# A block transpose of values, moved along VectorE's queue in a multi-query attention layer

## The chip, the cores and the metric

The kernel runs on one core of one Trainium2 chip. A core has engines that run side by side, each with its own queue of instructions that it takes in order: TensorE (PE, matrix products; its weight loads are shown as PEld), VectorE (DVE), ScalarE (ACT), GpSimd (POOL) and SyncE (SP), which here issues nearly all transfers. The engines tell each other by semaphores when something is done. The metric is device time in microseconds (us) of one execution; the runs before lie within 0.16 us of each other, so tenths of a microsecond can be read.

## What is computed

`x` holds 64 batches of 128 tokens with 512 numbers each. Each token row is normalised; 16 query heads of 64 numbers are projected from it, and one pair of keys and values that all heads share. A null key and value, taken from `cond`, stands ahead of the others. Scores get a bias and two masks, go through a softmax, weigh the values, are projected back, normalised and added to `x`.

```python
xn = layernorm(x, g_in)
q = (xn @ Wq).reshape(b, n, H, DH).transpose(0, 2, 1, 3) * scale
kv = xn @ Wkv
k, v = (kv[..., :DH], kv[..., DH:])
...
sim = jnp.einsum('bhid,bjd->bhij', q, k)
sim = sim + bias
...
attn = jax.nn.softmax(sim, axis=-1)
out = jnp.einsum('bhij,bjd->bhid', attn, v)
out = out.transpose(0, 2, 1, 3).reshape(b, n, INNER)
out = out @ Wo
return layernorm(out, g_out)
```

The outer function returns `x` plus this.

## The kernel before

**Groups and pairs.** Batches are worked in groups of four (`g`, 16 of them) and in pairs (`d`, 32 of them, with batches `a = 2d` and `b = 2d + 1`). The schedule is written out by hand: each engine gets its instructions in the order in which the Python code calls the helpers. For each pair there is a `turn(d)`, which makes the scores of the pair and the values products of the pair before (`p = 2d - 2`), and then a `body(d)`, for d from 1 to 29. The last two pairs have `turn_end` and `body_end`.

**What a body does.** Body d works on four things at once. It runs the softmax of pair d (`exps` on ScalarE, `rinv` on VectorE, `scale` on GpSimd, then `blocks_T`, a large transpose on VectorE that makes the weights of the values products). It projects the output of pair d - 1 (`out_product`, `out_part`), and normalises, adds and stores the output of pair d - 2 (`pair_stats`, `pair_nmr`, `pair_norm`, `pair_gain`, `pair_residual`). It makes keys, values and queries of the group after the next scores, `g = d // 2 + 1`: an even body (`h = 0`) does the first half of this group, an odd body (`h = 1`) the second. And it prepares token rows of group `g + 1`, as long as there is one (`norm_stats`, `norm_nmr`, `norm_apply`, `tokens_T`, then `tokens_out` and `tokens_in`, a round through DRAM that leaves the tokens transposed in `xT`).

**Keys and values.** `kv_pair` (L363) makes keys and values of two batches in one product `pkv`, keys in the lower 64 partitions, values in the upper. `kv_pair_out` reads it: VectorE takes the values into `vT` (L380), ScalarE the keys into `kT` (L390), and SP copies the keys to the other 64 partitions (L396). When the second pair of a group is through, `values_T(g)` brings the four batches' values into rows: VectorE transposes `vT` in blocks of 32 by 32 into `vb` (L401), SP writes `vb` to DRAM in two transfers (`vd`, L406) and reads it back in four (`vr`, L411). `values` (L781, tiles `po`) reads `vr` in the turns of that group.

**Queries.** The query projection is done by a scheme of seven products in place of eight: `product(g, f, k, ...)` (L515) makes product k for feature block f; both blocks f0 and f1 of a body use the same two rooms in PSUM, `pa` and `pc`. Products 1, 6, 7, 4 go into `pa` one on top of the other, products 5 and 3 into `pc`; between them, `keep` (ScalarE, L527) and `q_out` (VectorE L536, or ScalarE L533) read what stands there. Product 5 opens a new tile in `pc` and so needs the last reading of the old one done. Product 2 is again split into seven small ones, `inner_product` (L581, tile `pl`), read by `inner_out` (VectorE, L597), from d = 2 on; body 1 makes product 2 as a whole instead, and then prepares the summed weights for the small ones in `weight_sums_inner` (L554).

**Order on VectorE in an odd body.** The values (L380), the transpose `vb` (L401), then the readings of the norms: `pair_nmr` (L919), `norm_stats` (L270 to L280); then score maxima, gains and residuals (L929, L932) with the query readings between them, `tokens_T` (L326), two readings of small products (L597), the reciprocal `rinv(a, 1)` (L701), two more readings, `blocks_T(a)` (L721) and so on. An even body has the same order without `vb`.

**Order on SP in an odd body.** Keys copy, `vd` twice, `vr` four times, two stores (L935), `xd` (L335), `xT` four times (L343), two `res` (L131), two `x` (L122).

Of the kernel before, what the change touches and what calls it, by code (L numbers as in the profile page):

```python
# [17 lines left out]
def kernel(  # L18
# [356 lines left out]
    def kv_pair_out(m, pkv):  # L375
        g, t = divmod(m, GB)
        if t == 0:
            vTs[g] = hp.tile([P, GB, N], FP, tag="kv", name=f"vT_{g}", bufs=1)
        two = slice(t, t + 2)
        nc.vector.tensor_scalar(  # L380
            vTs[g][V_ROWS, two],
            pkv[V_ROWS].rearrange("p (t n) -> p t n", t=2),
            nkv[V_ROWS],
            None,
            ALU.subtract,
        )
        src = pkv[K_ROWS].rearrange("p (t i q) -> p t i q", t=2, i=NQ)
        out = kT[K_ROWS, :, two].rearrange("p i t q -> p t i q")
        for at, to, n in ((0, 0, 2), (3, 2, 1), (2, 3, 1)):
            nc.scalar.activation(  # L390
                out[:, :, to : to + n],
                src[:, :, at : at + n],
                AF.Identity,
                bias=nkv_neg[K_ROWS],
            )
        nc.sync.dma_start(out=kT[V_ROWS, :, two], in_=kT[K_ROWS, :, two])  # L396

    def values_T(g):

        vb = hp.tile([P, GB * NQ, Q], FP, tag="vb", name=f"vb_{g}", bufs=1)  # L400
        nc.vector.transpose(  # L401
            vb[V_ROWS], vTs[g][V_ROWS].rearrange("p t (j q) -> p (t j) q", q=Q)
        )
        vd = dp.tile([Q, GB * NQ, DH], FP, tag="vd", name=f"vd_{g}")
        for at in range(0, DH, Q):
            nc.sync.dma_start(  # L406
                out=vd[:, :, at : at + Q], in_=vb[DH + at : DH + at + Q]
            )
        vr[g] = hp.tile([P, GB, NQ, DH], FP, tag="vr", name=f"vr_{g}")
        for s in range(NQ):  # L410
            nc.sync.dma_start(  # L411
                out=vr[g][s * Q : (s + 1) * Q].rearrange("p t j d -> p (t j) d"),
                in_=vd,
            )
# [114 lines left out]
    def q_out(g, c, h, tag, name=None):  # L529
        o = q_part(g, c, h)  # L530
        p = prod[tag].rearrange("p (t h i) -> p t h i", t=2, h=2)
        if name is None:
            nc.scalar.copy(o, p)  # L533
        else:
            k = kept.pop(name).rearrange("p (t h i) -> p t h i", t=2, h=2)
            nc.vector.tensor_tensor(o, p, k, ALU.add)  # L536
# [10 lines left out]
    def weight_sums_inner():  # L547
        for o, p, m, op in (
            (r1, d21, d22, ALU.add),
            (r2, r1, d11, ALU.subtract),  # L550
            (r4, d12, r2, ALU.subtract),
            (r3, d11, d21, ALU.subtract),
        ):
            nc.vector.tensor_tensor(o, p, m, op)  # L554
# [10 lines left out]
    def inner_product(g, h, k):  # L565

        if k == 1:
            inner[g, h] = ps_w.tile([P, 4, N], FP, tag="w", name=f"pl_{g}_{h}")
        lo = xT[g][:, 0 : GB // 2]
        x = xL.get(g)  # L570
        t1, t3, t2, t4 = (x if x is None else x[:, i] for i in range(4))
        w, t, at = {
            1: (d11, lo[:, 0, HK], 0),
            2: (d12, lo[:, 0, KC - 1], 2),
            3: (r4, lo[:, 1, KC - 1], 1),
            4: (d22, t4, 0),
            5: (r1, t1, 1),
            6: (r2, t2, 0),
            7: (r3, t3, 0),
        }[k]  # L580
        nc.tensor.matmul(  # L581
            inner[g, h][:, at],
            w[:, h],
            t,
            start=k == 1,
            stop=True,
            skip_group_check=k != 1,
        )

    def inner_out(g, h, f, t, at, name=None):  # L590

        o = q_part(g, 2 * h + f, 0)[:, t]
        p = inner[g, h][:, at].rearrange("p (h i) -> p h i", h=2)
        k = o
        if name is not None:
            k = kept[name].rearrange("p (t h i) -> p t h i", t=2, h=2)[:, t]
        nc.vector.tensor_tensor(o, p, k, ALU.add)  # L597
# [80 lines left out]
    def exps(b, hf, lo=0, hi=R8):  # L678
        if hf == 0 and lo == 0:
            rsum[b] = small.tile([P, 2, R8], FP, tag="rsum", name=f"rsum_{b}")  # L680
        for k in range(lo, hi):
            row = S[b][:, k, WITH_NULL[hf]]
            nc.scalar.activation(  # L683
                row,
                row,
                AF.Exp,
                bias=nmax[b][:, hf, k : k + 1],
                accum_out=rsum[b][:, hf, k : k + 1],
            )
# [8 lines left out]
    def rinv(b, hf, lo=0, hi=R8):  # L698
        if lo == 0:
            rinvs[b, hf] = small.tile([P, R8], FP, tag="rinv", name=f"rinv_{b}_{hf}")  # L700
        nc.vector.reciprocal(rinvs[b, hf][:, lo:hi], rsum[b][:, hf, lo:hi])  # L701

    def scale(b, hf, lo=0, hi=R8):
        sv = S[b][:, lo:hi, KEYS[hf]]
        nc.gpsimd.tensor_tensor(  # L705
            sv,
            sv,
            rinvs[b, hf][:, lo:hi].unsqueeze(2).broadcast_to([P, hi - lo, sv.shape[2]]),
            ALU.mult,
        )  # L710
# [534 lines left out]
    def body(d):  # L1245

        a, b, p, l = 2 * d, 2 * d + 1, 2 * d - 2, 2 * d - 4
        g, h = d // 2 + 1, d % 2
        q, soft = g < NG, d > 0
# [20 lines left out]
            token_sum(g, 3)  # L1270
        if q:
            kv_pair_out(g * GB + 2 * h, pkv)
            if h == 1:
                values_T(g)
        if h == 0 and g + 1 < NG:
            load_mask(g + 1)
        if ln:
# [102 lines left out]
        if deep:  # L1380
            inner_product(g, h, 7)
            inner_out(g, h, 1, 1, 0, "p1")
            inner_out(g, h, 1, 1, 1)
        elif q:
            q_out(g, f1, 0, "w", "p1")
            weight_sums_inner()
        if soft:
            exps(a, 1, 4)
            rinv(a, 1)
            scale(a, 1)  # L1390
            exps(b, 1, 0, 2)
# [184 lines left out]
    for d in range(1, PAIRS - 2):  # L1576
        turn(d)
        body(d)
# [42 lines left out]
```

## Time and profile before

| | us |
|---|---|
| median of three runs | 1029.53 (1029.39 to 1029.55) |
| the profiled execution, its own time | 1029.77 |
| its span | 1027.9 |
| 16 transposes `vb`, each | 0.71 |

The page gives the busy time of each engine and the chain of work that ended last. The lists of groups give the mean duration of an instruction by line and operation. The chain in order of time has a start, a length and what ran; the timelines have a start, a duration, the engine, the line, what is written and read, and in brackets how long the engine stood idle before and who released it. Successive instructions of VectorE overlap slightly, so a start can lie a little ahead of the end before it. Busy time of PE is modelled at its ends: a product that is held back shows as a longer piece of the chain, not as idle time.

### The profile page before, as it was taken

To read this page: it belongs to the slowest core of one execution; us is meant where nothing else is said; L and a number is where in the kernel's file an instruction comes from. 1 tells how busy PE (TensorE), PEld (TensorE's weight loads), DVE (VectorE), ACT (ScalarE), POOL (GpSimd) and SP (SyncE) were. 2 spreads that over 40 slices of the span, in tenths; PEclk is the share of its full clock that TensorE was granted. 3 is DMA by queue.
4 is the path that set the end of the run, shared out by engine and by line. 5 is a ranking of instruction groups with operands and counts; after the bars stand their busy time and mean duration, and the time that the engine had idled before them with its cause. 6 is when DMAs were issued, how large, how long until landed. Compare 5 with 4: busy or idle time off the path is not lost.

```text
span 1027.9 us, 31287 instructions
## 1 busy us (share of the span) xinstructions
PE 1018.8 (99%) x12345; PEld 899.6 (88%) x12345; DVE 799.0 (78%) x1774; ACT 699.1 (68%) x2805; POOL 745.2 (72%) x579
## 2 busy tenths in 40 slices
PE   9999999999999999999999999999999999999997
PEld 9888888888888888888888888888888888888886
DVE  6877777877778877788777788777888777877697
ACT  5766678666678666786666786666776667856582
POOL 4997768686686857758677686776868678586676
PEclk9999999999999999999999999999999999999999
DMA  6514152141522315233141421415223151230211
GB/s 212 144 56 127 66 152 87 53 129 64 163 77 92 99 59 167 68 108 114 45 150 67 134 99 49 140 63 158 83 76 108 60 172 69 94 90 25 82 63 63
DMA packets 73834, 100.85 MB, mean 98 GB/s; under 512 B 32212, under 2 KB 36056, under 8 KB 71896
## 3 DMA queue, kind: packets, MB, share of 16 engines
q1 hardware_dynamic: 73392, 98.47, 30.8%
q8 instruction: 96, 1.57, 0.6%
q14 instruction: 50, 0.41, 0.1%
q10 hardware_dynamic: 296, 0.40, 0.1%
HBM read 63.19 MB, written 33.55 MB: 94 GB/s over the span
## 4 chain that ended last, share of the span: by engine, by line
PE 97%; DVE 1%; POOL 1%; issue 0%; POOLq 0%; DVEq 0%
PE pa L515 20%; PE pyX L868 19%; PE pyY L868 10%; PE pc L515 10%; PE po L781 7%; PE pkv L363 6%; PE pyw L868 5%; PE pl L581 4%; PE pq L450 3%; PE ps L652 3%; PE sc_X L652 2%; PE sc_Y L652 2%; PE py_s L868 1%; PE sc_a L652 1%; PE sc_w L652 1%; PE busy L1453 1%
## 5 line engine op out<-in xcount | busy, mean ns | idle before, releaser
L683 ACT ACTIVATE s<-s,nmax 128x65 f32<-128x65 f32 (+1 forms) x1024 | 372.0, 367 | 62.4 <-DVE nmax L674 62.4
L705 POOL TENSOR_TENSOR s<-s,rinv 128x512 f32<-128x512 f32 (+1 forms) x132 | 190.8, 1448 | 151.0 <-DVE rinv L701 151.0
L617 POOL TENSOR_TENSOR s<-biasp,mneg 128x1552 f32<-128x1552 f32 (+1 forms) x65 | 205.9, 3171 | 51.2 <-DVE s L667 38.2
L683 ACT ACTIVATION_READ_ACCUMULATOR s<-s,nmax 128x1 f32 x1024 | 194.6, 190 | 0.0
L533 ACT COPY qT<-pa 128x256 f32<-128x256 f32 x59 | 22.0, 373 | 147.2 <-PE pa L515 147.2
L674 DVE TENSOR_REDUCE nmax<-s 128x8 f32<-128x1032 f32 (+1 forms) x128 | 121.4, 949 | 0.1
L515 PE MATMUL pa<-xS,wq 128*128 128x256 f32 x472 | 121.2, 379 | 0.0
L721 DVE STREAM_TRANSPOSE sb<-s 128x1536 f32<-128x1536 f32 (+1 forms) x68 | 113.5, 1672 | 2.0 <-POOL s L705 2.0
L868 PE MATMUL pyX<-wT,oT 128*128 128x256 f32 x464 | 109.7, 379 | 0.0
L868 PE MATMUL pyX<-wo,oT 128*128 128x256 f32 x464 | 109.7, 379 | 0.0
L515 PEld LDWEIGHTS pa<-xS,wq 128*128 128x128 f32 x472 | 87.2, 190 | 11.1 <-issue 0.2
L868 PEld LDWEIGHTS pyX<-wo,oT 128*128 128x128 f32 x464 | 86.0, 190 | 10.5
L868 PEld LDWEIGHTS pyX<-wT,oT 128*128 128x128 f32 x464 | 85.9, 190 | 10.6
L848 POOL TENSOR_TENSOR oT<-oT 128x512 f32<-128x512 f32 x64 | 80.6, 1277 | 3.9 <-PE pyw L868 1.6
L781 PE MATMUL po<-sb,vr 32*64 32x256 f32 (+1 forms) x4064 | 81.4, 300 | 0.0
L781 PEld LDWEIGHTS po<-sb,vr 32*64 32x64 f32 x4064 | 70.9, 130 | 8.4 <-issue 5.3
L597 DVE TENSOR_TENSOR qT<-pl,kp 128x128 f32<-128x128 f32 x112 | 31.2, 279 | 58.6 <-PE pl L581 56.0
L800 ACT ACTIVATE oT<-po,nv 128x512 f32<-128x512 f32 (+1 forms) x127 | 73.7, 654 | 0.1
L536 DVE TENSOR_TENSOR qT<-pc,ku 128x256 f32<-128x256 f32 x118 | 48.5, 411 | 32.5 <-PE pc L515 18.1
L281 POOL TENSOR_TENSOR rstd<-rstd,nhalf 128x1 f32<-128x1 f32 x64 | 35.1, 555 | 52.5 <-DVE rstd L280 43.6
L363 PE MATMUL pkv<-xT,wkv 128*128 128x256 f32 x256 | 63.3, 391 | 0.0
L527 ACT COPY ku<-pa 128x256 f32<-128x256 f32 x118 | 43.4, 368 | 28.3 <-PE pa L515 23.8
(186 smaller groups left out, 2419.2 us busy)
## 6 DMA issues: line engine op xcount, KB each, us to landing
res<-in_x_dram SPq DMA_DIRECT2D x64, 256.0 KB
x<-in_x_dram SPq DMA_DIRECT2D x63, 256.0 KB
out_dram<-y SPq DMA_DIRECT2D x63, 256.0 KB
xd<-xb SPq DMA_DIRECT2D x14, 1024.0 KB
xT<-xd SPq DMA_DIRECT2D x56, 256.0 KB
vr<-vd SPq DMA_DIRECT2D x64, 128.0 KB
kT<-kT SPq DMA_DIRECT2D x32, 64.0 KB
vd<-vb SPq DMA_DIRECT2D x32, 64.0 KB
```

The lines of the kernel that those rows point to most:

```text
L363: nc.tensor.matmul(pkv, wkv[:, kc, :], xT[g][:, t : t + 2, kc, :], start=(kc == 0), stop=(kc == KC - 1),)
L515: nc.tensor.matmul(prod[tag], w[:, kc, f * P : (f + 1) * P], t[:, :, kc, :], start=(start and kc == 0), stop=(kc == HK - 1), skip_group_ch ...
L617: nc.gpsimd.tensor_tensor(S[b][:, :, keys], biasp[:, :, keys], mneg[:, t, keys] .unsqueeze(1) .broadcast_to([P, R8, keys.stop - keys.start ...
L652: nc.tensor.matmul(home[r][u * DH : (u + 1) * DH, f, :], qT[g, f, t // 2][rows, t % 2, hf, u], kT[rows, 0 : nk // Q, t, :], start=True, st ...
L674: nc.vector.tensor_reduce(nmax[b][:, hf], S[b][:, :, WITH_NULL[hf]], AX.X, ALU.max, negate=True)
L683: nc.scalar.activation(row, row, AF.Exp, bias=nmax[b][:, hf, k : k + 1], accum_out=rsum[b][:, hf, k : k + 1],)
L705: nc.gpsimd.tensor_tensor(sv, sv, rinvs[b, hf][:, lo:hi].unsqueeze(2).broadcast_to([P, hi - lo, sv.shape[2]]), ALU.mult,)
L721: nc.vector.transpose(sbs[b][:, :, lo:hi].rearrange("p j e q -> p e j q"), S[b][:, lo:hi, 1 : ROW - 1].rearrange("p e (j k) -> p e j k", k=Q),
L781: nc.tensor.matmul(po[s][rows, to : to + n], vr[g][quad, t, PLACE[j], :], sb[quad, slots, r * NF : (r + 1) * NF, :], start=(turn == 0), st ...
L800: nc.scalar.activation(to, src, AF.Identity, bias=nv2)
L848: eng.tensor_tensor(o, a, b, op)
L868: nc.tensor.matmul(prod[key], h[:, c, :], w[:, c, :], start=(start and c == 0), stop=(c == HC - 1), skip_group_check=not start,)
```

## The change

The call of `values_T(g)` moves within `body`. It stood directly behind `kv_pair_out`; now it stands behind the two readings of small product 7 (or, in body 1, behind `weight_sums_inner`), ahead of `exps(a, 1, 4)`, `rinv(a, 1)` and `scale(a, 1)`. Its transpose takes that place in VectorE's queue, and its six transfers come behind the two `x` loads in SP's. The call for group 0, ahead of the first turn, stays. Nothing else is changed.

```diff
@@ body
         if q:
             kv_pair_out(g * GB + 2 * h, pkv)
-            if h == 1:
-                values_T(g)
         if h == 0 and g + 1 < NG:
             load_mask(g + 1)
@@ body
         elif q:
             q_out(g, f1, 0, "w", "p1")
             weight_sums_inner()
+        if q and h == 1:
+            values_T(g)
         if soft:
             exps(a, 1, 4)
             rinv(a, 1)
```

## The prediction

> **What bounds the kernel now.** I read the page first: how full each engine is, and what the chain that ended last consists of.
>
> ```profile
> span 1027.9 us, 31287 instructions
> PE 1018.8 (99%) x12345; PEld 899.6 (88%) x12345; DVE 799.0 (78%) x1774; ACT 699.1 (68%) x2805; POOL 745.2 (72%) x579
> PE 97%; DVE 1%; POOL 1%; issue 0%; POOLq 0%; DVEq 0%
> ```
>
> TensorE is busy for 1018.8 of 1027.9 us and makes up 97% of the chain. A change on VectorE can pay only where it shortens something that PE itself counts as busy. So I cut the steady state into whole periods, from one keys product to the next, and asked for the busy time of each engine in them (columns: window, length, then each engine's busy time with its count, PE clock, DMA share, GB/s).
>
> ```profile
> 160.24:191.47 31.23, 31.23 (x384) 27.63 (x383) 24.29 (x56) 22.27 (x89) 23.55 (x20) 1.00 0.16 56
> 191.47:222.86 31.39, 31.39 (x383) 27.70 (x383) 24.90 (x57) 21.35 (x87) 21.75 (x16) 1.00 0.47 142
> 222.86:254.09 31.23, 31.23 (x384) 27.62 (x383) 24.29 (x56) 22.29 (x89) 23.54 (x20) 1.00 0.16 57
> ```
>
> PE is busy all through, at full clock. The first and third windows start with an even body (d = 4, 6), the second with an odd one (d = 5). Both issue the same PE work, yet the odd one takes 0.16 to 0.17 us longer. VectorE executes one instruction more there (57 against 56, 24.90 against 24.29 us): `values_T`. The chain of waits, in order of time, says where the extra time sits (start, length, what).
>
> ```profile
> 172.78 0.86 PE pc L515 x4
> ...
> 141.38 1.04 PE pc L515 x4
> ...
> 204.00 1.04 PE pc L515 x4
> ...
> 892.86 1.04 PE pc L515 x4
> ...
> 955.48 0.87 PE pc L515 x4
> ```
>
> It is one piece: product 5 of the second feature block on `pc`, 0.86 us in an even body and 1.04 in an odd one. From 141.38 (d = 3) to 892.86 (d = 27) every odd body has a piece of 1.03 or 1.04, thirteen in all. Body 29 (955.48) has none; it reads no more tokens, so VectorE has less in front. Body 1, with its own branch, has none either. What holds the piece is in the instruction timelines.
>
> ```profile
> 170.88 0.68 DVE L932 TENSOR_TENSOR y<-yn,res 128x512 f32<-128x512 f32 x1
> 171.73 0.42 DVE L536 TENSOR_TENSOR qT<-pc,ku 128x256 f32<-128x256 f32 x1 [0.17 <-PE pc L515]
> 172.61 1.03 PE L515 MATMUL pc<-xS,wS 128*128 128x256 f32 x4
> ...
> 193.96 0.71 DVE L401 STREAM_TRANSPOSE vb<-vT 64x512 f32<-64x512 f32 x1
> 202.84 0.68 DVE L932 TENSOR_TENSOR y<-yn,res 128x512 f32<-128x512 f32 x1
> 203.44 0.41 DVE L536 TENSOR_TENSOR qT<-pc,ku 128x256 f32<-128x256 f32 x1
> 203.91 1.13 PE L515 MATMUL pc<-xS,wS 128*128 128x256 f32 x4
> ```
>
> Product 5 opens a new tile in the slot of `pc`, so it waits until `q_out` (L536) has read the old one. In the even body `q_out` waits 0.17 us for PE: VectorE is early. In the odd body it stands directly behind the residual L932 with no idle time: VectorE is late, ends at 203.85, and PE starts at 203.91.
>
> **The change part by part.** *The early place (13 odd bodies, d = 3 to 27).* The transpose leaves the place at 193.96. Everything behind it on VectorE comes up to 0.71 us earlier, until it meets an input. That is the queue of the even body, whose `q_out` starts at 171.73; one 31.23 us period later is 202.96, against 203.44 now. In the even body it ends at 172.15, 0.46 us before PE comes at 172.61, so the stall goes: 1.04 - 0.86 = 0.17 to 0.18, and 31.39 - 31.23 = 0.16 from the windows. I take 0.17: 13 x 0.17 = 2.2 us gained. Nothing can yield more here, since the period of the even body has the same PE work.
>
> *The new place in these bodies.* The transpose now follows the second reading behind small product 7 and precedes the reciprocal `rinv(a, 1)`.
>
> ```profile
> 173.58 0.29 DVE L597 TENSOR_TENSOR qT<-pl,qT 128x128 f32<-128x128 f32 x1
> 174.59 0.20 DVE L701 RECIPROCAL rinv<-rsum 128x8 f32<-128x8 f32 x1 [0.72 <-ACT s L683]
> 174.87 1.91 POOL L705 TENSOR_TENSOR s<-s,rinv 128x1024 f32<-128x1024 f32 x1 [1.19 <-DVE rinv L701]
> 177.12 1.77 DVE L721 STREAM_TRANSPOSE sb<-s 128x1536 f32<-128x1536 f32 x1
> ...
> 205.82 0.20 DVE L701 RECIPROCAL rinv<-rsum 128x8 f32<-128x8 f32 x1 [0.25 <-ACT s L683]
> 211.16 0.42 DVE L536 TENSOR_TENSOR qT<-pc,ku 128x256 f32<-128x256 f32 x1 [0.46 <-ACT ku L527]
> ```
>
> In the even body, VectorE is idle for 0.72 us before that reciprocal, because ScalarE's exponentials are not done; the reciprocal comes at 174.59 + 31.23 = 205.82 by either body. A transpose of 0.71 us fits into 0.72, so I charge nothing. Without that cover the reciprocal would be 0.7 us late at most. Behind it GpSimd's scaling ends at 176.78, and the large transpose that needs it starts at 177.12, so 0.3 us more is absorbed. What is left, 0.4 us, would move a `q_out` that now waits 0.46 us for ScalarE (at 211.16), and PE would still not see it. Body 29, which reads no tokens, has more room still.
>
> *Body 1.* Its branch has no small products; the call stands behind `weight_sums_inner`. VectorE is not idle there.
>
> ```profile
> 78.55 0.42 DVE L536 TENSOR_TENSOR qT<-pc,ku 128x256 f32<-128x256 f32 x1 [2.17 <-PE pc L515]
> 82.00 0.20 DVE L701 RECIPROCAL rinv<-rsum 128x8 f32<-128x8 f32 x1
> 84.21 1.78 DVE L721 STREAM_TRANSPOSE sb<-s 128x1536 f32<-128x1536 f32 x1 [2.02 <-POOL s L705]
> 86.32 0.37 DVE L536 TENSOR_TENSOR qT<-pc,ku 128x256 f32<-128x256 f32 x1
> ...
> 86.98 1.03 PE L515 MATMUL pc<-xT,wS 128*128 128x256 f32 x4
> ...
> L515 PE MATMUL pc<-xS,wS x236: 379/379/483, 52.0 to 956.0; 128*128 128x256 f32 x118
> ```
>
> What the early place saves here is lost in the 2.17 us that VectorE waits before 78.55. From there to 82.00 it runs without a gap, so the transpose pushes the reciprocal by 0.63 us (0.71 less the 0.08 by which L932 and `q_out` overlap at 203.44) to 0.71 us. The reciprocal releases GpSimd's scaling, this the large transpose at 84.21, and behind it, without a gap, stand a copy, a reciprocal and the `q_out` at 86.32. That ends at 86.69 now and would end at 87.32 to 87.40. PE wants to add product 3 onto the same `pc` at 86.98; with the 0.06 us seen at 203.85 to 203.91 it starts 0.40 to 0.48 us late. A matmul that has waited also lasts longer: 483 ns at most against 379, so 0.10 more. Together 0.50 to 0.58; I take 0.55 us lost, once. The lower bound, should something release the chain that I do not see, is zero.
>
> The Trainium skill, "TensorE: Matmul & The Clock Gate", section "Single matmul latency", puts the fixed part of a lone matmul at about 166 ns, which speaks for a dearer restart than my 0.10. By it, as an estimate, body 1 would cost 0.06 more and the sum come to 1.6 us of gain. The trace disagrees: of the 0.17 us of a stall 0.07 is then a late start, and 0.07 + 0.166 would be 0.24, which no odd body shows.
>
> *The six transfers.* `vd` twice and `vr` four times move on SP's queue from behind the keys copy to behind the token loads.
>
> ```profile
> 195.51 1.30 SPq L406 DMA_DIRECT2D vd<-vb  x2
> 198.39 1.74 SPq L411 DMA_DIRECT2D vr<-vd  x4
> ...
> 205.09 0.33 SPq L335 DMA_DIRECT2D xd<-xb  x1
> 208.98 1.76 SPq L343 DMA_DIRECT2D xT<-xd  x4
> ...
> 211.74 1.23 SPq L122 DMA_DIRECT2D x<-in_x_dram  x2
> 226.14 0.67 SPq L396 DMA_DIRECT2D kT<-kT  x1
> ...
> 251.64 2.45 PE po L781 x123
> ```
>
> `vr` of this body is first read at 251.64, in the values products two turns later. SP stands free from 212.97 to 226.14. The two `vd` would be issued by 214.3. Ahead of them are 2 MB of `xT`, `res` and `x`; 1 MB of `xd` took until 208.98, 3.9 us, so at most 8 us. `vr` then goes out before 224 and lands some 27 us before its use. If it held SP longer, the keys copy would be late first, and its reader too is two turns away. I charge nothing. Stores, `xd` and `xT` lose six transfers ahead of them, which PE does not see.
>
> *New waits on PE.* The changed program's instruction order shows that in the turns that first read a group's `vr` (turns 5 to 29, thirteen of them) three matmuls gain a wait on a transfer, which earlier waits used to cover; turn 3 gains one. Turn 1 already has waits on all four.
>
> ```profile
> 63.78 2.45 PE po L781 x122
> ...
> L781 PEldq EVENT_SEMAPHORE  x4: 51/51/51, 63.0 to 63.5; - x4
> ...
> 189.02 2.45 PE po L781 x123
> ```
>
> Turn 1, whose queue worked off four wait instructions of 51 ns ahead of them, and turn 5 take the same 2.45 us. So a wait that is already satisfied costs less than the last digit, and I charge nothing; the upper bound is a broken stream, 0.10 us of restart and 0.05 of issue each.
>
> *Sum.* -2.2 + 0.55 = -1.65 us against the profiled execution's 1029.77 us (span 1027.9): 1028.1. The median of the runs, 1029.53, is 0.24 below that execution, so the forecast is 1027.9 us.
>
> **The rivals.** *Body 1 loses nothing.* Then 1029.53 - 2.2 = 1027.3. For it: one unseen body, a chain of five steps. Against it: none of these steps has idle time that isn't waiting for the one before.
>
> *The waits that take the cover's place (slower).* If the three new waits break PE's stream in the thirteen turns, each costs 0.15: 13 x 0.45 = 6 us, and 1027.9 + 6 = 1033.8. It is slower than before from 0.13 us a turn on, one broken wait, and by over 0.2% from 0.29. Against it stand the 2.45 us of turn 1.
>
> *The change does not free the tile.* If something else holds `q_out` where it is (a norm reading, ScalarE's normalised row), the stall stays and only body 1 speaks: 1029.53 + 0.55 = 1030.1. Against it: the even body, which has the same queue without the transpose and no stall.
>
> **How the numbers follow.** The forecast 1027.9 has 0.44, body 1 for nothing 0.34 (1027.3), the stall that stays, in whole or in part, 0.11 (1028.5 to 1030.1), broken waits 0.11 (up to 1033.8). About 0.2%, 2.06 us, is what a measurement of this kernel can tell from no change. Of the four, only body 1 for nothing is faster by that much: 0.34. The forecast is faster by 0.16%, which with the stall that stays makes "within" 0.55; broken waits 0.11 slower. The range takes the first two whole and the lower part of the third: 1027.0 to 1029.0.
>
> **What would show it.** Odd and even periods of equal length; `pc` pieces of 0.86 us in all thirteen odd bodies; a `pc` piece near 87 us that has grown by half a microsecond; `rinv(a, 1)` of the odd bodies with next to no idle time before it; values products of 2.45 us in turns 5 to 29; SP free again before 226. Wrong is the forecast if odd periods stay at 31.39, if a new wait stands ahead of the values products, or if body 1's pieces are as before.

## The result, and the profile after

| | us |
|---|---|
| median before, 17 runs on the same chip | 1029.62 (1029.39 to 1030.42) |
| median after, 17 runs | 1027.55 (1027.23 to 1028.13) |
| ratio | 0.998, 95% interval 0.9972 to 0.9987 |
| forecast | 1027.9, range 1027.0 to 1029.0 |

The change makes the kernel faster by 2.07 us, 0.2%; 1.65 were forecast. Over 17 runs the times of before span 1.03 us, not the 0.16 us of its first three, so the smaller terms below are read from the traces, one for each kernel. The head of the page of after, then the windows of after, cut from one values product `po` to the next: body 1 first, then bodies 4 and 5 (window, length, busy time of PE, PEld, DVE, ACT, POOL with their counts, PE clock, DMA share, GB/s).

```profile
span 1025.8 us, 31271 instructions
PE 1016.4 (99%) x12345; PEld 898.9 (88%) x12345; DVE 800.4 (78%) x1774; ACT 697.4 (68%) x2805; POOL 744.7 (73%) x579
```

```profile
63.67:95.78 32.11, 31.66 (x385) 27.50 (x388) 22.07 (x47) 19.79 (x85) 26.04 (x16) 1.00 0.36 103
158.22:189.45 31.23, 31.23 (x391) 27.62 (x393) 24.30 (x56) 22.27 (x89) 23.98 (x22) 1.00 0.24 80
189.45:220.67 31.22, 31.22 (x390) 27.62 (x392) 24.99 (x57) 21.25 (x87) 21.28 (x16) 1.00 0.41 120
```

Body 1 of before, cut in the same way:

```profile
63.78:95.17 31.39, 31.39 (x384) 27.58 (x387) 22.08 (x47) 19.79 (x85) 26.59 (x17) 1.00 0.42 122
```

The odd period of before, 31.39 us, has become 31.22 and equals the even one. Body 1 went the other way, from 31.39 to 32.11 us, 0.72 more; PE is busy for 31.66 us of it, so here 0.45 us show as idle time of PE and not as a longer piece. The products on `pc` show both at once. From the instructions of the product line in after (min/median/max in ns, first and last start):

```profile
L515 PE MATMUL pc<-xS,wS x236: 379/379/382, 51.9 to 954.3; 128*128 128x256 f32 x118
L515 PE MATMUL pc<-xT,wS x236: 379/379/483, 58.8 to 962.5; 128*128 128x256 f32 x118
```

Product 5 (`xS`), which reached 483 ns before, never does so now: none of them has waited. The 483 has moved to product 3 (`xT`), and the waits of PE have one such case, 0.4 us long:

```profile
PE pc L515 <- DVE qT L536: 0.4, 1, 0.4
```

*The balance of the two profiled executions.* Body 1 begins 0.11 us earlier (63.67 against 63.78; over all ten traces of this study it begins between 63.23 and 63.78, so this is no effect of the change) and costs 0.72 more. From its end to the last values products it is 1006.12 - 95.17 = 910.95 us before and 1004.48 - 95.78 = 908.70 after: 2.25 gained in the thirteen odd bodies, 0.17 each. Two rows of the chain of waits at the very end give one more term; before first, then after:

```profile
1006.12 2.24 PE po L781 x69
...
1009.01 1.97 PE pyc L868 x8
```

```profile
1004.48 1.56 PE po L781 x64
...
1007.02 1.97 PE pyc L868 x8
```

From the last values products to the output product behind them it is 2.89 us before and 2.54 after: 0.35 us that I had not foreseen. What follows is 0.04 shorter (18.82 us to the end of the span against 18.86; the traces have the spans as 1025.84 and 1027.87). The sum, -0.11 + 0.72 - 2.25 - 0.35 - 0.04 = -2.03, is the difference of the spans.

*The odd body at its new place.* Instructions of VectorE in body 5 of after:

```profile
203.39 0.42 DVE L536 TENSOR_TENSOR qT<-pc,ku 128x256 f32<-128x256 f32 x1 [0.17 <-PE pc L515]
...
205.56 0.71 DVE L401 STREAM_TRANSPOSE vb<-vT 64x512 f32<-64x512 f32 x1
206.30 0.20 DVE L701 RECIPROCAL rinv<-rsum 128x8 f32<-128x8 f32 x1
208.37 0.29 DVE L597 TENSOR_TENSOR qT<-pl,kp 128x128 f32<-128x128 f32 x1 [1.87 <-PE pl L581]
```

`q_out` at 203.39 now waits 0.17 us for PE, as it did in the even body of before: VectorE is early. `rinv(a, 1)` stands behind the transpose with 0.03 us of gap, and the idle time behind it, 1.87 us, swallows the rest.

### The profile page after: what moved, and what is told of

Read it like the earlier page. It is cut to its first block, busy times and chain, and to the rows that moved or that the text cites. A ratio compares the mean times of both kernels' runs of the same rounds, so it can differ in the third digit from the quotient of the medians.

```text
span 1025.8 us, 31271 instructions
## 1 busy us (share of the span) xinstructions
PE 1016.4 (99%) x12345; PEld 898.9 (88%) x12345; DVE 800.4 (78%) x1774; ACT 697.4 (68%) x2805; POOL 744.7 (73%) x579
## 4 chain that ended last, share of the span: by engine, by line
PE 97%; DVE 1%; POOL 1%; issue 0%; POOLq 0%; DVEq 0%; ACT 0%
PE pa L515 20%; PE pyX L868 19%; PE pyY L868 10%; PE pc L515 10%; PE po L781 7%; PE pkv L363 6%; PE pyw L868 5%; PE pl L581 4%; PE pq L450 3%; PE ps L652 3%; PE sc_X L652 2%; PE sc_Y L652 2%; PE py_s L868 1%; PE sc_a L652 1%; PE busy L1453 1%; PE sc_w L652 1%
```

## The experiments

All are compared with the kernel before on the same chip; its medians in these comparisons lay between 1029.62 and 1029.80 us. A period is the stretch from one `po` to the next, as above.

### Body 1 alone, in both directions

Is body 1 a loss of its own, and is the gain of the odd bodies independent of it? The first kernel is the one after, with body 1's call back at its old place (`deep` is true for the bodies from 2 on that make a group):

```diff
+            if d == 1:
+                values_T(g)
...
-        if q and h == 1:
+        if deep and h == 1:
             values_T(g)
```

> The changed kernel, with the transpose of body 1 alone put back to its old place. Theory (the early transpose held the second block's product 5 in 13 odd bodies; the late one costs body 1 0.72 us, since turn 1 to turn 2 took 32.11 us instead of 31.39): all odd periods 31.23, period 1 31.39 again, 1027.55 - 0.72 = 1026.8 us. Rival (the gain comes from elsewhere and the longer period 1 is made up for later): 1027.5, as the changed kernel.

Measured: 1026.69 us (1026.61 to 1026.94), ratio 0.9972 (0.9961 to 0.9983). Its windows, body 1 and body 5:

```profile
63.60:94.99 31.39, 31.39 (x384) 27.62 (x387) 22.07 (x47) 19.77 (x85) 26.22 (x16) 1.00 0.43 120
...
188.67:219.90 31.23, 31.23 (x391) 27.67 (x393) 25.00 (x57) 21.25 (x87) 21.27 (x16) 1.00 0.41 120
```

The second is the kernel before, with only body 1's call moved:

```diff
-            if h == 1:
+            if h == 1 and d > 1:
                 values_T(g)
...
+        if d == 1:
+            values_T(g)
```

> The kernel before, with the transpose of body 1 alone at the new place. Theory: odd periods from body 3 on stay at 31.39 to 31.40, period 1 becomes 32.11, 1029.62 + 0.72 = 1030.3 us. Rival (body 1's loss is made up for later): 1029.6.

Measured: 1030.47 us (1030.13 to 1030.84), ratio 1.0007 (0.9998 to 1.0015). The interval of the times does not exclude 1. The windows show the loss, again body 1 and body 5:

```profile
63.44:95.54 32.10, 31.66 (x384) 27.53 (x387) 22.08 (x47) 19.78 (x85) 26.02 (x16) 1.00 0.35 103
...
189.40:220.80 31.40, 31.40 (x390) 27.75 (x393) 24.90 (x57) 21.34 (x87) 21.28 (x16) 1.00 0.45 138
```

The two add up: 0.71 us lost where body 1 alone is moved, 0.17 gained per odd body where all but body 1 are. Body 1 costs something, so the rival that had it for nothing falls.

### One place that is free in every body

If the loss in body 1 is the reciprocal's delay, a place directly behind the reciprocal and its scaling must be free there, as VectorE then waits 2.02 us for GpSimd (the row at 84.21 of before).

```diff
-        if q and h == 1:
-            values_T(g)
         if soft:
             exps(a, 1, 4)
             rinv(a, 1)
             scale(a, 1)
+        if q and h == 1:
+            values_T(g)
+        if soft:
             exps(b, 1, 0, 2)
```

> The changed kernel, with the call of values_T one step further back, behind the reciprocal and the scaling of (a, 1), in every odd body. Theory: in body 1 the reciprocal is back near 81.9 us and the transpose stands in the 2 us in which VectorE waits for GpSimd, so period 1 is 31.39; in the others it stands in the 1.9 us ahead of the next small product; odd periods 31.23; 1026.8 us. Rival (any late transpose in body 1 moves the chain reciprocal, scaling, large transpose): period 1 near 32.1, 1027.5.

Measured: 1026.78 us (1026.49 to 1027.18), ratio 0.9972 (0.9962 to 0.9983). VectorE in body 1, and the window of body 1:

```profile
81.76 0.20 DVE L701 RECIPROCAL rinv<-rsum 128x8 f32<-128x8 f32 x1
81.99 0.71 DVE L401 STREAM_TRANSPOSE vb<-vT 64x512 f32<-64x512 f32 x1
83.97 1.78 DVE L721 STREAM_TRANSPOSE sb<-s 128x1536 f32<-128x1536 f32 x1 [1.28 <-POOL s L705]
```

```profile
63.55:94.93 31.38, 31.38 (x384) 27.57 (x386) 22.16 (x47) 19.78 (x85) 26.45 (x16) 1.00 0.36 104
```

The transpose takes 0.74 of the 2.02 us, 1.28 are left, and body 1 is as long as before the change. Its median is 2.84 us below that of before, and its slowest run (1027.18) is below the fastest of after (1027.23, from another comparison): one rule for all bodies, without the loss in body 1.

### The suspected cost doubled, at the old place and at the new

The transpose is executed twice for every group but the first, in the kernel before:

```diff
-        nc.vector.transpose(
-            vb[V_ROWS], vTs[g][V_ROWS].rearrange("p t (j q) -> p (t j) q", q=Q)
-        )
+        for _ in range(2 if g else 1):
+            nc.vector.transpose(
+                vb[V_ROWS], vTs[g][V_ROWS].rearrange("p t (j q) -> p (t j) q", q=Q)
+            )
```

> The kernel before, with the transpose done twice in a row at its old place (the same values written twice, for all groups but the first). Theory: VectorE is back to back from there to the reading of pc in the 13 bodies from 3 to 27, so the second transpose goes into PE's wait in full, 0.74 to 0.82 us each, 9.6 to 10.7 in all; bodies 1 and 29 have 2.17 and 0.93 us of idle time on the way and lose nothing; 1039.2 to 1040.3 us, pc pieces of 1.8 us. Rival (the place of the transfers is what matters, not the transpose): 1029.6.

Measured: 1039.27 us (1039.08 to 1039.59), ratio 1.0094 (1.008 to 1.0107). Body 1 and body 5:

```profile
63.59:94.98 31.39, 31.39 (x384) 27.58 (x387) 22.56 (x48) 19.89 (x85) 26.27 (x16) 1.00 0.43 121
...
189.57:221.72 32.15, 31.91 (x391) 27.54 (x392) 25.63 (x58) 21.25 (x87) 21.28 (x16) 1.00 0.44 134
```

Each of the thirteen odd bodies pays the second transpose in full, 32.15 - 31.40 = 0.75 us. From the transpose to the second block's `q_out` VectorE has no idle time, and that `q_out` starts 10.76 us after the reading of the values (L380) where it was 10.01 before, 0.75 later. So the old place really is on the path there, and the rival by which something else holds `q_out` falls. Body 1 pays nothing, because of the 2.17 us of idle time ahead of its `q_out`.

Two parts of the expectation failed. The `pc` pieces were to be 1.8 us and none is longer than 1.13. ScalarE in body 5, and then the pieces of PE in which the time sits:

```profile
196.31 0.78 ACT L927 ACTIVATE yn<-y,nmro,rstdo 128x512 f32<-128x512 f32 x1 [0.77 <-DVE nmro L920]
```

```profile
198.69 1.13 PE pa L516 x4
...
203.08 1.01 PE pc L516 x4
...
205.22 1.13 PE pc L516 x4
```

The late `pair_nmr` on VectorE holds ScalarE's normalised row `yn`, and behind that stands the copy `ku` of product 6, which product 7 on `pa` needs. Product 7 starts 1.23 us after product 5 (0.86 before) and takes 0.10 more: 0.47. The other 0.28 are on `pc`, 0.15 in the first block's product 3 and 0.13 at the second block's product 5. And body 29, which was to lose nothing, loses 0.47 us in the same way: its product 7 starts 1.23 us after product 5 (957.88 and 959.11; 0.87 before), 0.10 longer. In sum 13 x 0.75 + 0.47, less 0.35 us at the end that are treated below, is 9.87, against 9.65 between the medians; body 1 begins 0.19 us earlier in this trace (63.59 against 63.78).

The same edit in the kernel after:

> The changed kernel with the transpose done twice in a row at its new place (the same values written twice, for all groups but the first). Theory (from body 3 on a delay of about 1.2 us of the reciprocal behind it does not reach PE): the reciprocal comes 0.74 us later than in the changed kernel, odd periods stay at 31.23; body 1 has no cover and loses 0.74 us more; 1027.55 + 0.74 = 1028.3 us. Rival (the cover at the new place is only the 0.7 us of idle time that one transpose fills): odd periods longer by 0.3 to 0.7 us, 1032 to 1037.

Measured: 1028.21 us (1028.14 to 1028.56), ratio 0.9986 (0.9977 to 0.9995). Its windows of body 1 and body 5, and VectorE in body 5:

```profile
63.42:96.27 32.85, 31.67 (x385) 27.50 (x388) 22.88 (x48) 19.78 (x85) 26.45 (x17) 1.00 0.36 104
...
189.95:221.18 31.23, 31.23 (x390) 27.64 (x394) 25.78 (x58) 21.25 (x87) 21.28 (x16) 1.00 0.41 120
```

```profile
206.06 1.45 DVE L402 STREAM_TRANSPOSE vb<-vT 64x512 f32<-64x512 f32 x2
207.54 0.20 DVE L702 RECIPROCAL rinv<-rsum 128x8 f32<-128x8 f32 x1
...
209.76 1.78 DVE L722 STREAM_TRANSPOSE sb<-s 128x1536 f32<-128x1536 f32 x1 [0.40 <-POOL s L706]
...
211.92 0.42 DVE L537 TENSOR_TENSOR qT<-pc,ku 128x256 f32<-128x256 f32 x1
```

At the new place the odd bodies carry even 1.45 us for nothing (31.23, as in after); the large transpose now waits 0.40 us for GpSimd, and the `q_out` behind it, which waited 0.46 us for ScalarE before, waits no more: the cover is used up there, not exceeded. Body 1 pays the second transpose in full, 32.85 - 32.11 = 0.74.

### The transfers alone

`values_T` is cut in two: the transpose stays early, the six transfers go to the new place.

```diff
+        vbs[g] = vb
+    def values_rows(g):
+        vb = vbs.pop(g)
         vd = dp.tile([Q, GB * NQ, DH], FP, tag="vd", name=f"vd_{g}")
...
+        if q and h == 1:
+            values_rows(g)
         if soft:
             exps(a, 1, 4)
```

> The kernel before with only the six transfers of values_T moved: the transpose stays at its old place, vd and vr are issued behind the x loads. Theory (the transfers' place and the waits that come with it on PE cost and bring nothing): odd periods 31.39 to 31.40 as before, values products 2.45 us in turns 5 to 29, 1029.6 us. Rival (the transfers out of the way of stores and tokens are the gain): odd periods near 31.23, 1027.3.

Measured: 1029.56 us (1029.43 to 1030.57), ratio 0.9999 (0.999 to 1.0008). The chain still has the long pieces of before, product 5 in body 5 among them (1.04 us before), and the values products are as they were; turn 5, the first to read `vr` of body 3, and the row of body 5:

```profile
188.82 2.45 PE po L788 x122
...
203.80 1.05 PE pc L522 x4
```

So the transfers, and PE's additional waits on them, neither cost nor bring anything. All of the change's effect comes with the transpose's place.

### The 0.35 us at the end

VectorE's last reading of `py_s` shows where they come from: before, and then after.

```profile
1003.13 0.43 DVE L898 TENSOR_TENSOR y<-py_s,kyp 128x256 f32<-128x256 f32 x1 [1.03 <-ACT s L683]
```

```profile
1001.13 0.42 DVE L898 TENSOR_TENSOR y<-py_s,kyp 128x256 f32<-128x256 f32 x1 [0.68 <-PE py_s L868]
```

VectorE is idle ahead of it in both, but in before for 0.35 us longer, with no releaser at that moment: of its inputs ScalarE's `kyp` was done at 1001.24 and PE's `py_s` at 1002.67, and the exponentials that the row names are none of them. The same hole is seen in the run that moves body 1 alone and in the one that moves the transfers alone, and not in the other four. In the traces of the three kernels that have the hole, 1983 records of VectorE (waits included) stand ahead of this reading. In the others it is 1969 (after, body 1 alone put back, behind the reciprocal), 1998 (doubled at the old place) or 1984 (doubled at the new place); the move leaves 14 waits fewer on VectorE. Theory A: it depends on how many instructions VectorE has had. To tell, small instructions are put into an idle stretch of VectorE in body 1, far from the end, 15 in the kernel before and 14 in the kernel after; they fill a tile that nothing reads.

```diff
+    tick = const.tile([P, 16], FP, name="tick")
...
+        if d == 1:
+            for i in range(15):
+                nc.vector.tensor_scalar(tick[:, i : i + 1], gin8[:, 0:1], 0.0, None, ALU.add)
         if out:
             out_sum(p, 3)
```

> The kernel before with 15 one-column instructions more on VectorE in body 1, where it waits 2 us for PE; they write a tile that nothing reads. It asks about the end of the kernel, where the reading of the last pair's product 7 starts 0.11 us after PE in the changed kernel and 0.46 us after it in the kernel before. Theory A (the 0.35 us hang on where that reading stands in VectorE's instruction stream, which 15 more instructions move as the doubled early transpose did): the reading starts 0.1 us after PE, all else as before, 1029.6 - 0.35 = 1029.3 us. Theory B (they hang on something else that the old place of the transpose brings, such as a store or a later engine): 0.46 us after PE, 1029.6.

> The changed kernel with 14 such instructions more in the same place, which puts the last reading at about the position in VectorE's stream that it has in the kernel before (14 waits fewer are queued ahead of it in the changed one). Theory A: the reading starts 0.46 us after PE again, 1027.55 + 0.35 = 1027.9 us. Theory B: 0.1 us, 1027.55.

Measured: 1029.54 us (1029.18 to 1030.14), ratio 0.9996 (0.9987 to 1.0005), with 15 in the kernel before; 1027.82 (1027.58 to 1028.38), ratio 0.9981 (0.9971 to 0.999), with 14 in the kernel after. The first median is 0.26 us below that of before beside it (1029.80), the second 0.27 above that of after (1027.55, from another comparison). Both are on the side that theory A expects, but within the spread; the times do not decide. The rows say more. The reading with 15 in the kernel before, then with 14 in the kernel after:

```profile
1002.79 0.42 DVE L899 TENSOR_TENSOR y<-py_s,kyp 128x256 f32<-128x256 f32 x1 [0.68 <-PE py_s L869]
```

```profile
1001.09 0.42 DVE L899 TENSOR_TENSOR y<-py_s,kyp 128x256 f32<-128x256 f32 x1 [1.03 <-ACT s L684]
```

The hole has gone from the kernel before (1006.13 to 1008.67, 2.54 us instead of 2.89) and has come into the kernel after (1004.08 to 1006.97, 2.89 instead of 2.54), while body 1 and the odd periods stayed as they were in each. So theory B falls: the old place of the transpose is not needed. The first now has 1998 records ahead of the reading, the second 1983. Over all ten traces the hole is there where exactly 1983 stand ahead (four) and absent with 1969, 1984 or 1998 (six), as theory A says. With one trace of each kernel and no other position tried, what VectorE does in these 0.35 us stays open. One lead: in the four traces with the hole, an 8 KB packet of queue q14, "instruction" on the page, begins 0.65 to 0.71 us behind the start of the reading; in the other six none begins from 2.8 us ahead of it to 1.5 us behind it. Whether that is the cause or a sign was not tried.

## Why the prediction came out as it did

**The early place: right.** Thirteen odd bodies at 0.17 us were to bring 2.2 us; the balance has 2.25. The transpose doubled there costs its full 0.75 us per body, so VectorE's queue is the path, as the chain of before said; that a delay of this size would reach PE first through ScalarE was not seen.

**The new place in these bodies: right.** It was to be free, with some 1.4 us of cover (0.72, 0.3 and 0.4). It is free, and two transposes are too.

**Body 1: the mechanism right, the size off.** The chain of waits of after shows the five steps that I named (reciprocal, GpSimd's scaling, large transpose, copy and reciprocal, `q_out`), one behind the other, and PE's product at the end:

```profile
82.31 0.41 ACT s L683 x2
...
82.73 0.21 DVE rinv L701
...
83.01 1.92 POOL s L705
...
84.95 1.78 DVE sb L721
86.73 0.31 DVE kyu L880
87.03 0.11 DVE rinv L701
87.14 0.30 DVE qT L536
...
87.49 1.13 PE pc L515 x4
```

Ahead of the reciprocal the chain names exponentials on ScalarE that end at 82.72, and not the transpose. That is a coincidence in time: they belong to batch b, the code places them behind this reciprocal, and those that it needs end at 81.28. In before the same exponentials of b end at 82.81, after the reciprocal's start at 82.00; with the transpose doubled they end at 82.47 and the reciprocal still comes only behind the transposes, at 83.22.

The term was 0.55 us and measured 0.72 (0.71 in the run that moves body 1 alone). The step that failed is "the transpose pushes the reciprocal by 0.63 us (...) to 0.71": I let it overlap its neighbour by 0.08 us, as L932 and `q_out` do, or at best follow without loss. VectorE in body 1, two rows of before and three of after:

```profile
81.66 0.42 DVE L554 TENSOR_TENSOR wq<-wq 128x256 f32<-128x256 f32 x1
82.00 0.20 DVE L701 RECIPROCAL rinv<-rsum 128x8 f32<-128x8 f32 x1
```

```profile
81.56 0.42 DVE L554 TENSOR_TENSOR wq<-wq 128x256 f32<-128x256 f32 x1
81.99 0.71 DVE L401 STREAM_TRANSPOSE vb<-vT 64x512 f32<-64x512 f32 x1
82.73 0.20 DVE L701 RECIPROCAL rinv<-rsum 128x8 f32<-128x8 f32 x1
```

Before, the reciprocal starts 0.34 us after the start of the instruction ahead of it, so the two overlap by 0.08. The transpose starts 0.43 after it, and the reciprocal 0.74 after the transpose: no overlap on either side. The queue grows by 0.43 + 0.74 - 0.34 = 0.83 us. With the 0.23 us that `q_out` had to spare (86.98 - 86.69 - 0.06) PE is late by 0.60; from 86.98 - 0.11 to 87.49 it is 0.62. The restart adds the 0.10 that I took (483 ns against 379). By the 166 ns that the Trainium skill has for the fixed part of a lone matmul ("TensorE: Matmul & The Clock Gate", "Single matmul latency"; given there for bf16, while these products are f32) it would be about 0.79, an estimate; the measured 0.72 stays with the row.

**The transfers and PE's waits: right in price, one cover thinner than I said.** SP was to be free again before 226. Its instructions in after, with start and length:

```profile
223.66 2.78 SPq L411 DMA_DIRECT2D vr<-vd  x4
226.54 0.64 SPq L396 DMA_DIRECT2D kT<-kT  x1
```

`vr` went out from 223.66 on, as estimated, but was done only at 226.44, and the keys copy stands directly behind it (226.14 in before). Its reader is two turns away, so nothing came of it; the run with the transfers alone says the same.

**The end of the kernel: not in the sum.** The 0.35 us there and the 0.17 missing in body 1 have opposite signs, and with 0.15 us of start and end, and 0.05 more in the odd bodies, they make up the difference between the 1.65 forecast and the 2.03 of the two traces (2.07 between the medians). That the forecast came as near as 0.35 us is in part luck: two errors worked against each other. Had body 1 been sized right and nothing else changed, the forecast would have been 1028.1.

Of the rivals, body 1 for nothing (1027.3) lay nearer to the measured 1027.55 than the forecast did, for a wrong reason: body 1 loses even more than I charged. Broken waits and a tile that isn't freed are ruled out by the windows.

## What to carry to other kernels

An instruction on an engine with slack still has a cheapest place: behind the instruction that releases another engine's work, not ahead of it, and in a stretch where its own engine waits for that work (here 2.02 us behind a reciprocal). Where one rule places it in bodies with different contents, look at each kind of body: one body of fifteen gave back a third of the gain. And to price an instruction in a gapless stretch, take the distance of starts that this very instruction has to its neighbours elsewhere in the trace, not its duration, and add the overlap that its new neighbours lose.

## What the hardware showed that I had not expected

The `vb` transpose (64 x 512) doesn't overlap its neighbours on VectorE: 0.71 us of duration took 0.83 of the queue, while the large transpose of 128 partitions starts 0.08 us before the instruction ahead has ended. At its old place the `vb` transpose took less, 0.74 us (1.27 from the start of L380 to that of L919 in body 5 of before, 0.53 in body 5 of after), since those two do not overlap without it either. Two rows of VectorE in body 5 of before:

```profile
208.32 0.28 DVE L597 TENSOR_TENSOR qT<-pl,qT 128x128 f32<-128x128 f32 x1
208.52 1.77 DVE L721 STREAM_TRANSPOSE sb<-s 128x1536 f32<-128x1536 f32 x1
```

Here the second starts at 208.52, the first ends at 208.60. Whether the 64 partitions or something else makes the difference was not tried.

VectorE can stand still for 0.35 us ahead of an instruction whose inputs are there: in four of ten traces, all four with that instruction at the same place in its queue. In a kernel whose changes bring a few tenths of a microsecond, that can pass for an effect of the change.
